# The end of a two-layer network on one core: last contexts kept in SBUF, the choice in two passes, eight groups of expert weights ahead, answers and tokens moved as groups end

## The chip, the cores and the metric

The kernel runs on one core of one Trainium2 chip. Its time is device time in microseconds (us) of one launch; "faster" and "slower" compare medians of such runs.

## What is computed

The input is four images of 64 x 64 positions with 128 channels, 4096 tokens an image. Two layers follow each other; the second has two parts, and the change lies at the end of the second part:

```python
x = x + L0(_gn(x))              # three selective scans (forward, backward, sliced)
t = _to_tokens(x)
t = t + L1_attn(_ln_t(t))       # attention, 16 heads of 8
t = t + L1_ffn(_ln_t(t))        # experts choose tokens
```

```python
# L1_attn, after q was made
scores = einsum('bhsd,bhtd->bhst', q, q) / sqrt(8); attn = softmax(scores)
attn_out = einsum('bhst,bhtd->bhsd', attn, q) @ w_comb.T + b_comb
x1 = _ln(x + attn_out, g1, beta1)
h = relu((cos(x1[..., :8]) * cos(ry_theta)) @ w1.T + b1)
return _ln(x1 + h @ w2.T + b2, g2, beta2)
# L1_ffn: 64 experts, each takes its 8 best tokens of an image
probs = softmax(x @ gate_w.T + gate_b, axis=1)      # over the tokens
vals, idx = top_k(probs, 8)
pooled = sum of the 8 tokens, weighted by vals
h = gelu([pooled, 1] @ weight1[e]); out = [h, 1] @ weight2[e]
outputs[idx] += out * vals
```

The expert weights are 64 x (128 x 512 + 512 x 128) numbers in float32, and each is used once.

## The kernel before, in words

The scans come first; their steps then run beside the attention of the image before. An image's attention is `Attention.loop`: a turn is a set j of four heads and a block qb of 512 queries, and in a turn 32 rounds go over 128 keys each. A round makes scores (L1013), takes their exponential on ACT (L1018), and adds the weighted values and the sum of the weights into `acc` (L1027). At the end of a turn `sums` copies `acc` to the tile `av` (L1036; two buffers), and three rounds later POOL's queue stores contexts (L1042) and denominators (L1045) to DRAM. Other work is put between the rounds by hand, through generators that yield where they may be interrupted. For the last image (index 3) the turns go block by block, and between the rounds stand, in this order: what follows image 2's attention, the expert biases, then for the pair of images 0 and 1 and for image 2 the experts' search, choice and gather, then the blocks 0 to 6 of image 3 (`after`), and a search over their logits. Only block 7 of image 3 remains when the loop ends.

`after` for a block: `shares` loads the denominators, inverts them (L1105) and stores them as shares (L1106). `first` loads the block's normed tokens (L1113), the contexts (L1115) and the shares spread over eight rows a head (L1117), multiplies (L1122), applies `w_comb` (L1130), norms (L893 to L899, with two small operations on POOL, L50 and L51), and stores x1. Then a sine (L1241), and `second`: x1 and t back from DRAM (L1146, L1148), transposes (L1153), h (L1171), fo (L1184), two norms, stores of t2 and xn (L1196, L1200), transposes (L1208), logits (L1222), which for this last block go straight into the tiles `prob` and `best` (L1226).

`choice` finds the eight best (L1321), takes the exponential of `prob` in place in four cuts with sums (L1331), replaces the eight best by -1 in a copy called `chosen` (L1335), and multiplies marks by exponentials (L1345): `chosen` then holds the weight where an expert chose a token and zero elsewhere. `gather` (`pool`) goes over blocks of 512 tokens, two at a time: load xn (L1352, SyncE's queue, four buffers), turn the weights by a matmul with a diagonal of the inverse sums (L1357), copy (L1363), pool (L1368), and add to `pooled` (L1374).

`answers`: groups of four experts, 16 groups of 2.1 MB of weights (L1385, L1388). A group is h (L1399), a copy on ACT (L1404), transposes (L1409), bias (L1412) and Gelu (L1417), o (L1422), and a copy into `o_all` (L1426). Two groups run side by side. Five groups are loaded ahead: one from POOL's queue before the last loop, three from ACT's queue as the loop ends, and one more from ACT's queue after block 7. A group that ends starts the load of the group five later from SyncE's queue. Twelve token tiles t (`DEEP`) are loaded from POOL's queue (L1455). After the last group the answers go to DRAM by image (L1473) and come back by expert (L1477), get bias and share, and `scatter` multiplies them with `chosen` for each block (L1491), adds t (L1498), and SyncE's queue writes the output (L1500); the next t load follows.

Of the kernel before, what the change touches and what calls it, by code (L numbers as in the profile page):

```python
# [34 lines left out]
QB = 512  # L35
F32R = mybir.dt.float32r


# [690 lines left out]
class Attention:  # L729
# [3 lines left out]
    def __init__(self, tc, ctx, w, gate, cols, ident, bank, dram, t1, w_out, scans, sz, x):  # L733
# [53 lines left out]
        self.u, self.q, self.v, self.context, self.total, self.t2 = {}, {}, {}, {}, {}, {}  # L787
        self.xn, self.logits, self.angled, self.whole, self.closed = {}, {}, {}, {}, {}
        self.lag, self.cut = 0, False
        self.round = column(nc, const, ROUND, "round"), column(nc, const, -ROUND, "minus_round")  # L790
# [172 lines left out]
    def loop(self, b, beside, by_block=False):  # L963
# [69 lines left out]
        def sums(j, qb, i):  # L1033

            av = self.mid.tile([P, QB], F32, tag="av", name=f"av_{b}_{j}_{qb}")
            (nc.vector.tensor_copy if by_block else nc.scalar.copy)(av, accs.pop((j, qb)))  # L1036
            cut = slice(qb * QB, (qb + 1) * QB)

            def store():
                for k in range(4):  # L1040
                    h = 4 * k + j
                    nc.gpsimd.dma_start(  # L1042
                        out=self.context[b][h * D : h * D + D, cut], in_=av[32 * k : 32 * k + D, :]
                    )
                nc.gpsimd.dma_start(  # L1045
                    out=self.total[b][qb].rearrange("(k j) t -> j k t", j=4)[j], in_=av[D::32, :]
                )
                if by_block and j == 3:
                    self.whole[b] = qb + 1

            later[i + 3] = store
# [22 lines left out]
    def after(self, b, gs=range(L // QB), to=None):  # L1074
# [173 lines left out]
        yield from flow((second(g) for g in gs), self.n, 32 // self.n)  # L1248


DEEP = 12


class Experts:
# [4 lines left out]
    def __init__(self, tc, ctx, ident, weight1, weight2, block, nb):  # L1259
# [14 lines left out]
        self.diagonal = const.tile([P, nb // 2, E], F32, name="diagonal")  # L1274
        self.found, self.ahead, self.rooms = {}, [], 0

# [17 lines left out]
    def search(self, images, blocks):  # L1294

        nc = self.nc
        rows = slice(images[0] % 2 * E, images[-1] % 2 * E + E)
        prob = self.const.tile([P, L], F32, tag="prob", name=f"prob_{images[0]}")
        best = self.some.tile([P, TOP + QB], F32, tag="best", bufs=1, name=f"best_{images[0]}")
        self.found[images] = rows, prob, best  # L1300
        while self.block.closed[images[-1]] < blocks:
            yield WAIT
        for b in images:
            own = slice(b % 2 * E, b % 2 * E + E)
            nc.sync.dma_start(out=prob[own, : blocks * QB], in_=self.block.logits[b][:, : blocks * QB])
        yield
        nc.vector.max(out=best[rows, :TOP], in_=prob[rows, : blocks * QB])
        yield
# [6 lines left out]
    def choice(self, images, blocks):  # L1315
# [10 lines left out]
        yield  # L1326
        nc.scalar.activation(top, top, AF.Exp, bias=low)
        total = some.tile([P, NC], F32, tag="total", name=f"total_{key}")[rows]
        for g in range(NC):
            cut = prob[rows, g * T : (g + 1) * T]  # L1330
            nc.scalar.activation(cut, cut, AF.Exp, bias=low, accum_out=total[:, g : g + 1])  # L1331
            yield

        w = self.chosen[key // 2][rows]
        nc.vector.match_replace(out=w, in_to_replace=top, in_values=prob[rows], imm_value=-1.0)  # L1335
        yield
# [3 lines left out]
        for b in images:  # L1340
# [3 lines left out]
            )  # L1344
        nc.vector.scalar_tensor_tensor(w, w, 0.0, prob[rows], ALU.is_lt, ALU.mult)  # L1345
        yield

    def pool(self, b, g):

        nc, bank, rows = self.nc, self.block.bank, slice(b % 2 * E, b % 2 * E + E)  # L1350
        x = self.some.tile([P, 4, C], F32, tag="x", bufs=4, name=f"x_{b}_{g}")
        nc.sync.dma_start(out=x, in_=self.block.xn[b][:, g * 4 : g * 4 + 4, :])  # L1352
        yield
# [11 lines left out]
        yield  # L1365
        ps = yield from bank.take(f"pool_{b}_{g}")
        for i in range(4):
            nc.tensor.matmul(ps[:, :E], x[:, i, :], wT[:, i, :], start=(i == 0), stop=(i == 3))  # L1368
# [9 lines left out]
    def gather(self, images):  # L1378
        yield from flow((self.pool(b, g) for b in images for g in range(NT // 4)), 2, 3)

# [11 lines left out]

    def answer(self, g, w, o_all, pool):

# [7 lines left out]
        yield  # L1402
        raw = pool.tile([P, 4, P], F32, tag="raw", name=f"hr_{g}")
        nc.scalar.copy(raw, ps.rearrange("r (p k) -> r k p", k=4))  # L1404
# [20 lines left out]
        yield  # L1425
        nc.vector.tensor_copy(o_all[:, g, :], ps[:, :C])  # L1426
        bank.leave()
# [7 lines left out]
    def prefetch(self, room, by):  # L1435

        pool, n = room
        for _ in range(n):
            self.ahead.append((self.weights(pool, len(self.ahead), by), pool))

    def answers(self, ctx, out):
        nc, tc, bank, nb = self.nc, self.tc, self.block.bank, self.nb
        once = ctx.enter_context(tc.tile_pool(name="e_once", bufs=1))
        pool = ctx.enter_context(tc.tile_pool(name="e_pool", bufs=2))
        deep = ctx.enter_context(tc.tile_pool(name="e_deep", bufs=DEEP))
        ng = E // GE
# [4 lines left out]

        def bring(i):
            b, g = tokens[i]
            t = deep.tile([P, 4, C], F32, tag="t", name=f"t_{b}_{g}")
            nc.gpsimd.dma_start(out=t, in_=self.block.t2[b][:, g * 4 : g * 4 + 4, :])  # L1455
            ts[b, g] = t

        o_all = once.tile([P, ng, C], F32, name="o_all")

        def group(g):  # L1460
            yield from self.answer(g, loaded.pop(g), o_all, pool)
            if g + n < ng:
                loaded[g + n] = self.weights(self.ahead[g % n][1], g + n, nc.sync)
            elif len(ts) < DEEP:
                bring(len(ts))

        yield from flow((group(g) for g in range(ng)), 2, 4)
        for i in range(len(ts), DEEP):
            bring(i)
        answers = [once.tile([P, C], F32, name=f"answer_{j}") for j in range(nb // 2)]  # L1470
        by_image = self.block.dram.tile([nb, E, C], F32, name="d_answers")
        for c in range(GE):
            (nc.sync, nc.scalar)[c % 2].dma_start(  # L1473
                out=by_image.rearrange("b (g c) o -> c b g o", c=GE)[c], in_=o_all[32 * c : 32 * c + nb]
            )
        for j in range(nb // 2):
            nc.sync.dma_start(out=answers[j], in_=by_image[2 * j : 2 * j + 2].rearrange("k e o -> (k e) o"))  # L1477
            nc.vector.tensor_add(answers[j], answers[j], self.bias_2)
            nc.vector.tensor_scalar_mul(answers[j], answers[j], self.share[:, j : j + 1])
        yield  # L1480

        def scatter(i):
# [13 lines left out]
            for (b, g), ps in zip(pair, banks):  # L1496
                t = ts.pop((b, g))
                nc.vector.tensor_add(t.rearrange("p t c -> p (t c)"), t.rearrange("p t c -> p (t c)"), ps)  # L1498
                bank.leave()
                nc.sync.dma_start(out=out[b].rearrange("(t p) c -> p t c", p=P)[:, g * 4 : g * 4 + 4, :], in_=t)  # L1500
                if i + DEEP < len(tokens):
                    bring(i + DEEP)
                i += 1
            yield
# [32 lines left out]
def tile_kernel(tc, ctx, x, in_proj_w, dirs, out_proj_w, attn, gate, weight1, weight2, out):  # L1537
# [82 lines left out]
    experts = Experts(tc, ctx, ident, weight1, weight2, block, nb)  # L1620
    experts.prefetch(experts.room(ctx, 1, "right"), nc.gpsimd)
    blocks = L // QB
    pairs = [(b, b + 1) for b in range(0, nb - 2, 2)] + [(nb - 2,), (nb - 1,)]
    with tc.manual_schedule():
# [6 lines left out]
            block.after(nb - 1, range(0, 4)), block.after(nb - 1, range(4, 6)), block.after(nb - 1, range(6, blocks - 1)),  # L1631
            experts.search(pairs[-1], blocks - 1),
        )
        block.loop(nb - 1, lambda i: last.turn(1.5, i % 3 > 0 or i > 830), True)
        last.rest()
        block.cut = False
    loop.close()
    with ExitStack() as end:
        block.bank = Bank(end.enter_context(tc.tile_pool(name="end_ps", bufs=7, space=PSUM)), 7)
        with tc.manual_schedule():  # L1640
            room = experts.room(end, 3)
            with ExitStack() as pieces:
                block.pieces_of(pieces, 1, opening=False)
                closing = block.after(nb - 1, range(blocks - 1, blocks), experts.rest(pairs[-1], blocks - 1))
                for i, _ in enumerate(closing):
                    if i == 2:
                        experts.prefetch(room, nc.scalar)
            experts.prefetch(experts.room(end, 1), nc.scalar)
            for _ in experts.choice(pairs[-1], blocks - 1):
                pass  # L1650
            for _ in experts.gather(pairs[-1]):
                pass
            for _ in experts.answers(end, out):
                pass
# [32 lines left out]
```

## Time and profile before

| | us |
|---|---|
| median of 3 runs | 11369.05 (11349.99 to 11371.47) |
| the profiled execution, its own time | 11359.39 |
| span of its trace | 11357.7 |
| busy: ACT, PE, DVE, POOL | 9991.9, 9864.2, 8267.2, 3757.7 |
| ACT's exponentials of the attention (L1018) | 7777.9 |
| last matmul of the attention ends | 11109.2 |
| first h of the answers starts (L1399) | 11229.2 |
| last addition of the output ends (L1498) | 11351.1 |
| moved from 11100 on | 53.04 MB |
| mean granted TensorE clock | 0.943 of full |

A row of a group of instructions gives the line, engine, operation, tiles out and in, shapes and count; then busy time and the mean of one in ns; then the engine's idle time just before them and what ended it. PE is TensorE's matmuls, PEld its weight loads; a float32 matmul is counted as two instructions. DVE is VectorE, ACT ScalarE, POOL GpSimd, and SPq, ACTq and POOLq are their queues of transfers. The granted clock is 1.00 at full speed. The time of the page is from the start of the span.

### The profile page before, as it was taken

To read this page: it belongs to the slowest core of one execution; us is meant where nothing else is said; L and a number is where in the kernel's file an instruction comes from. 1 tells how busy PE (TensorE), PEld (TensorE's weight loads), DVE (VectorE), ACT (ScalarE), POOL (GpSimd) and SP (SyncE) were. 2 spreads that over 40 slices of the span, in tenths; PEclk is the share of its full clock that TensorE was granted. 3 is DMA by queue.
4 is the path that set the end of the run, shared out by engine and by line. 5 is a ranking of instruction groups with operands and counts; after the bars stand their busy time and mean duration, and the time that the engine had idled before them with its cause. 6 is when DMAs were issued, how large, how long until landed. Compare 5 with 4: busy or idle time off the path is not lost.

```text
span 11357.7 us, 182956 instructions
## 1 busy us (share of the span) xinstructions
PE 9864.2 (87%) x68358; PEld 3270.5 (29%) x68358; DVE 8267.2 (73%) x8405; ACT 9991.9 (88%) x10828; POOL 3757.7 (33%) x3891
## 2 busy tenths in 40 slices
PE   6697782888999889999998898999998999999995
PEld 2233331222222222222222222222222223333323
DVE  7999987888888987999998979988999221111212
ACT  4576672999999999999999999999999999989992
POOL 5887773323323223334233124243331110000000
PEclk8898895999999999999999999999999999999997
DMA  7888887556566665665656655656555332222225
GB/s 200 235 253 228 231 239 206 147 144 156 140 155 164 178 171 140 158 164 136 156 140 172 185 158 153 156 140 153 148 146 156 119 99 71 76 71 83 76 64 187
DMA packets 900978, 1747.50 MB, mean 154 GB/s; under 512 B 203150, under 2 KB 443846, under 8 KB 899830
## 3 DMA queue, kind: packets, MB, share of 16 engines
q1 hardware_dynamic: 764414, 1468.11, 48.4%
q0 software_dynamic: 93856, 156.41, 4.8%
q10 hardware_dynamic: 41816, 111.28, 3.4%
q8 instruction: 537, 8.80, 0.3%
q14 instruction: 355, 2.91, 0.1%
HBM read 1379.76 MB, written 355.47 MB: 153 GB/s over the span
## 4 chain that ended last, share of the span: by engine, by line
PE 37%; ACT 25%; issue 14%; DVE 12%; DMA 10%; POOL 1%; SPq 1%; ACTq 0%; DVEq 0%; POOLq 0%
PE acc L1027 21%; ACT e L1018 20%; PE s L1013 10%; DVE h L576 5%; DMA delta<-d_delta 4%; DMA du<-d_du 2%; PE cv L415 2%; DVE dB L566 1%; ACT dA L557 1%; ACT delta L557 1%; PE y L614 1%; PE fo L1184 1%; PE h L1171 1%; PE xd L431 1%; DMA B<-d_bc 0%
## 5 line engine op out<-in xcount | busy, mean ns | idle before, releaser
L1018 ACT ACTIVATE e<-s 128x1024 f32<-128x1024 f32 x8192 | 7777.9, 1105 | 233.1 <-PE s L1013 221.3
L1027 PE MATMUL acc<-e,val 128*32 128x512 f32 x32768 | 5255.2, 616 | 106.7 <-ACT av L1036 94.0
L1013 PE MATMUL s<-qm,key 32*128 32x512 f32 x16384 | 2648.4, 500 | 588.5 <-ACT e L1018 558.4
L1013 PEld LDWEIGHTS s<-qm,key 32*128 32x128 f32 x16384 | 1013.8, 184 | 4448.8 <-issue 2490.0
L578 POOL COPY ends<-h 128x1 f32<-128x1 f32 x1152 | 1292.6, 1123 | 2332.1 <-DVE h L576 2318.1
L566 DVE TENSOR_TENSOR dB<-du,B 128x1024 f32<-128x1024 f32 x960 | 1216.0, 1267 | 450.8 <-PE y L614 224.7
L1027 PEld LDWEIGHTS acc<-e,val 128*32 128x32 f32 x32768 | 972.6, 109 | 1608.4 <-issue 787.9
L576 DVE TENSOR_TENSOR_SCAN h<-dA,ends,dB 128x1024 f32<-128x1024 f32 x576 | 1350.4, 2344 | 110.9 <-ACT dA L557 70.7
L557 ACT ACTIVATE dA<-delta,A 128x1024 f32<-128x1024 f32 x768 | 935.6, 1218 | 421.4 <-DMA delta<-d_delta 373.7
L576 DVE TENSOR_TENSOR_SCAN h<-delta,ends,du 128x1024 f32<-128x1024 f32 x432 | 1012.3, 2343 | 127.4 <-ACT delta L557 64.8
L583 POOL TENSOR_TENSOR hC<-h,C 128x1024 f32<-128x1024 f32 x384 | 1001.1, 2608 | 160.2 <-PE y L614 85.1
L557 ACT ACTIVATE delta<-delta,A 128x1024 f32<-128x1024 f32 x768 | 937.4, 1221 | 21.6 <-DMA d_du<-u 7.1
L587 DVE TENSOR_TENSOR du<-h,C 128x1024 f32<-128x1024 f32 x576 | 701.1, 1217 | 0.1
L587 DVE TENSOR_TENSOR dB<-h,C 128x1024 f32<-128x1024 f32 x576 | 701.0, 1217 | 0.0
L566 DVE TENSOR_TENSOR du<-du,B 128x1024 f32<-128x1024 f32 x576 | 690.6, 1199 | 6.0 <-DMA B<-d_bc 5.9
L1042 POOL DMA_DIRECT2D d_ctx<-av x512 | 260.2, 518 | 1020.8 <-DVE av L1036 647.0
L415 PE MATMUL cv<-xn,conv 128*128 128x512 f32 x1024 | 472.6, 615 | 41.8 <-DVE xn L346 31.7
L608 POOL DMA_DIRECT2D d_du<-x_delta x272 | 157.2, 578 | 1012.9 <-DVE x_delta L607 951.8
L576 DVE TENSOR_TENSOR_SCAN h<-dA,dB 128x1024 f32<-128x1024 f32 x192 | 438.7, 2285 | 40.7 <-ACT dA L557 30.4
L614 PE MATMUL y<-dB,sel 128*32 128x256 f32 x4608 | 378.5, 401 | 9.5 <-DVE xT L1211 5.1
L576 DVE TENSOR_TENSOR_SCAN h<-delta,du 128x1024 f32<-128x1024 f32 x144 | 328.8, 2283 | 67.4 <-issue 34.5
L614 PE MATMUL y<-hC,sel 128*32 128x256 f32 x3072 | 239.8, 443 | 147.9 <-DVE o L630 144.6
(246 smaller groups left out, 7198.1 us busy)
## 6 DMA issues: line engine op xcount, KB each, us to landing
delta<-d_delta SPq DMA_DIRECT2D x768, 512.0 KB
du<-d_du SPq DMA_DIRECT2D x632, 512.0 KB
key<-d_q SPq DMA_DIRECT2D x352, 256.0 KB
du<-d_du ACTq DMA_DIRECT2D x136, 512.0 KB
B<-d_bc SPq DMA_DIRECT2D x96, 512.0 KB
C<-d_bc SPq DMA_DIRECT2D x96, 512.0 KB
us<-d_u SPq DMA_DIRECT2D x384, 128.0 KB
y<-d_y SPq DMA_DIRECT2D x192, 256.0 KB
```

The lines of the kernel that those rows point to most:

```text
L415: nc.tensor.matmul(banks[2 * m + g], w["conv"][:, k, m * P : (m + 1) * P], reads(k, g), start=(k == 0), stop=(k == 3))
L557: nc.scalar.activation(tiles["delta", s], t, AF.Exp, scale=A)
L566: nc.vector.tensor_mul(tiles["du", s], du, spread[order, c, "B", j % 2])
L576: nc.vector.tensor_tensor_scan(h, dA, dB, first, ALU.mult, ALU.add)
L578: nc.gpsimd.tensor_copy(ends[order, c][:, at : at + 1], h[:, T - 1 :])
L583: nc.gpsimd.tensor_mul(tiles["du", s], h, spread[order, c, "C", j % 2])
L587: nc.vector.tensor_mul(dB, h, spread[order, c, "C", j % 2])
L614: nc.tensor.matmul(y[32 * g : 32 * g + 32, : T // 4], self.sel[:, j // 2, :], hC[:, 256 * g : 256 * g + 256], start=(j == 0), stop=(j == 3),)
L1013: nc.tensor.matmul(s_ps[:, k, :], keys[f"{i // 4}"][rows, cut].bitcast(F32R), queries[j, qb][rows, :].bitcast(F32R), start=True, stop=True,)
L1018: nc.scalar.activation(e, s_ps, AF.Exp, scale=1.0 / math.sqrt(D))
L1027: nc.tensor.matmul(accs[j, qb][32 * k : 32 * k + 32, :], v[:, k * VW : k * VW + 32], es[i][k // 2][:, k % 2, :], start=(kc == 0), stop=(kc ...
L1042: nc.gpsimd.dma_start(out=self.context[b][h * D : h * D + D, cut], in_=av[32 * k : 32 * k + D, :])
```

## The change

All of it concerns the last image's end, except that the choice for the other images changes its steps too.

- The contexts of image 3's block 7 are no longer stored: `sums` keeps the four `av` tiles (now four buffers). `combs` makes four copies of `w_comb` whose rows stand as the heads stand in `av`; `divide(j)` sums and spreads a tile's denominators by matmuls, inverts and multiplies in place. `combs` and `divide(0..2)` run between the rounds of the loop.
- `ending` replaces `after` for block 7: one pass without DRAM in between, activation tables loaded early, and 31 matmuls (`warm`) into a spare bank that nothing reads.
- `choice` writes exponentials to `chosen` and marks `prob`, and the marks are applied block by block as `pool` begins. `final`, for image 3, does the replacement beside a first set of exponentials that only give sums (into PSUM), and a second set in place; it turns weights one block ahead and sums all blocks in one bank.
- Weight groups 1 to 3 are loaded from SyncE's queue after the last division, 4 to 6 after `ending`, 7 after `final`. `prob` and `best` have a pool of their own that is given up for group 7.
- In `answers` three groups run side by side. As a group ends, four transfers from POOL's queue move its rows to their place in `answers` (for the last group two of them from ACT's). From group 8 on the room of a group's weights takes eight token tiles, from SyncE's queue; all 32 are loaded this way. The output leaves from SyncE's and ACT's queues in turn.

```diff
 def sums(j, qb, i):
+    if by_block and qb == L // QB - 1:
+        self.kept[j] = av
+        return
...
+def divide(self, j):
+    for i, cut in enumerate(halves):
+        for k in range(4):
+            one = self.ident[:, 32 * k + D : 32 * k + D + 1].to_broadcast([P, 32])
+            nc.tensor.matmul(ps[rows, cut], one, av[:, cut], start=True, stop=True)
+    for cut in halves:
+        nc.vector.reciprocal(r[:, cut], ps[:, cut])
+        nc.vector.tensor_mul(av[:, cut], av[:, cut], r[:, cut])
...
+def warm(self, n, by):
+    for i in range(n):
+        self.nc.tensor.matmul(self.spare, self.ident, by, start=True, stop=True)
...
+def ending(self, b, to, by, prefetch):
+    yield from self.divide(3)
+    prefetch()
+    nc.vector.tensor_add(u, u, spread("b_comb"))
+    for k in range(4):
+        for j in range(4):
+            nc.tensor.matmul(ps[:, at], self.kept[j][:, at], self.comb[:, j, :], start=(j == 0), stop=(j == 3))
+    self.warm(8, by)
...
+    self.warm(9, by)
+    yield from self.norm(u, u, f"x2{b}_{g}")
...
+    nc.tensor.matmul(ps[rows], self.gate, xT, start=True, stop=True)
+    self.warm(14, by)
...
+def final(self, images, blocks, by):
+    nc.vector.match_replace(out=w, in_to_replace=top, in_values=prob[rows], imm_value=GONE)
+    for g in range(n):
+        ps = yield from bank.take(f"exp_{g}")
+        nc.scalar.activation(ps[rows], prob[rows, cuts[g]], AF.Exp, bias=low, accum_out=total[:, g : g + 1])
+    for g in range(n):
+        nc.scalar.activation(prob[rows, cuts[g]], prob[rows, cuts[g]], AF.Exp, bias=low)
...
+    yield from turn(0)
+    for g in range(n):
+        if g + 1 < n:
+            yield from turn(g + 1)
+        x = self.xs.pop((b, g))
+        for i in range(4):
+            nc.tensor.matmul(sums[:, :E], x[:, i, :], wTs[g][:, i, :], ...)
+        if g + 4 < n:
+            self.tokens(b, g + 4)
...
 def group(g):
-    yield from self.answer(g, loaded.pop(g), o_all, pool)
+    o = pool.tile([P, C], F32, tag="o", name=f"os_{g}")
+    yield from self.answer(g, loaded.pop(g), o, pool)
+    for b in range(nb):
+        at = b % 2 * E + g * GE
+        by = (nc.gpsimd, nc.scalar)[b % 2] if g == ng - 1 else nc.gpsimd
+        by.dma_start(out=answers[b // 2][at : at + GE, :], in_=o[b::32, :])
     if g + n < ng:
         loaded[g + n] = self.weights(self.ahead[g % n][1], g + n, nc.sync)
-    elif len(ts) < DEEP:
-        bring(len(ts))
+    else:
+        bring(self.ahead[g % n][1], g)
...
-yield from flow((group(g) for g in range(ng)), 2, 4)
+yield from flow((group(g) for g in range(ng)), 3, 2)
```

## The prediction

> **What bounds the kernel now.** I read the page's rows by slices first, then the end of the run in stretches of 10 us, then the chain of waits in that stretch, then the groups by line. The page's slices (284 us each):
>
> ```profile
> PE   6697782888999889999998898999998999999995
> ACT  4576672999999999999999999999999999989992
> PEclk8898895999999999999999999999999999999997
> GB/s 200 235 253 228 231 239 206 147 144 156 140 155 164 178 171 140 158 164 136 156 140 172 185 158 153 156 140 153 148 146 156 119 99 71 76 71 83 76 64 187
> ```
>
> Up to the last slice ACT is full: the attention's exponentials (L1018, 7777.9 us) pace the run, and the change leaves nearly all of that alone. In the last slice ACT falls to 2 tenths and PE to 5. The change lives there: from the last matmul of the attention, at 11109.2, to the end of the span at 11357.7 are 248.5 us. Stretches of it (columns: length, busy time and instructions of PE, weight loads, DVE, ACT, POOL; granted clock; DMA share; GB/s):
>
> ```profile
> 11110.00:11120.00 10.00, 0.00 (x0) 0.00 (x0) 0.00 (x0) 0.00 (x0) 2.60 (x5) 0.72 1.00 349
> ...
> 11180.00:11190.00 10.00, 0.00 (x0) 0.00 (x0) 5.75 (x6) 4.15 (x8) 0.00 (x0) 0.50 0.99 362
> ...
> 11220.00:11230.00 10.00, 8.56 (x37) 7.31 (x40) 1.66 (x5) 0.00 (x0) 0.00 (x0) 0.50 0.00 0
> ...
> 11250.00:11260.00 10.00, 6.68 (x103) 3.18 (x105) 2.66 (x5) 3.12 (x6) 0.00 (x0) 1.00 1.05 387
> ...
> 11300.00:11310.00 10.00, 1.08 (x32) 0.81 (x32) 0.29 (x1) 0.63 (x1) 0.00 (x0) 0.77 0.10 13
> ```
>
> No one limit holds. Until 11230 it is a chain of latencies with the clock at half; in the experts' answers the transfers are full (387 GB/s); around 11305 nothing runs. The chain of waits (start, us, what):
>
> ```profile
> 11112.19 5.45 DMA d_sum<-av
> 11118.20 4.93 DMA x<-d_un
> 11124.22 5.64 DMA d_share<-sum
> 11130.37 3.43 DMA part<-d_share
> ...
> 11265.50 9.02 DMA w<-in_L_ffn_weight_dram
> ```
>
> The first four are round trips through DRAM for one 512-token block; the last is the answers waiting for weights. And the gather's groups, from the groups by line of this stretch (busy, mean ns | idle before):
>
> ```profile
> L1368 PE MATMUL pool<-wT,x 128*128 128x64 f32 x64 | 15.7, 427 | 4.1 <-DVE wT L1363 4.1
> L1357 PE MATMUL wt<-diagonal,chosen 64*128 64x64 f32 x64 | 15.7, 424 | 18.3 <-DVE chosen L1345 18.3
> ```
>
> **Part one: from the last context to the last block's logits.** Before, from the copy of the last sums (L1036, 11109.23) to `low` (L1325, ending 11177.75) are 68.5 us. Removed are the stores, loads and shares between 11109.92 and 11133.99, 24.1 us. Added in their place: eight matmuls that sum and spread the denominators, four at a time side by side, half of them ahead of DVE (0.7 us, from the answers' h of the same packing, 0.9 to 1.0 us for twice the columns); two reciprocals of 128x256 (the same shape took 1.75 us in L1105) and two multiplications (0.42); b_comb added (0.69). The combination has 16 matmuls instead of 4: at the transposes' 0.66 us for four at full clock 2.6 us, at the old row's 2.05 us for four at half clock 8.2 us; half of them lie on the path, 1.3 to 4.1.
>
> Behind that the rows of before repeat: a norm is 1.75 (statistics) + 1.43 (POOL) + 1.12, spreads are 0.7 each, h was 7.19 us and fo 5.83 us mostly at half clock. L1137 and L1138 (1.4) move behind the sine. With a full clock (h 3.6, fo 2.6) I add up: first halves divided and combined by 11116.3, norm 11121.5, sine 11123.5, h 11128.9, fo 11132.4, two norms with their spreads 11143.7, logits 11147.6, `low` 11148.6. I put 3 us on this for a clock that sags between, so 11151.5: **26 us gained**. If it is half throughout, 9 us more of matmul time.
>
> The fillers (8, 9 and 14 matmuls of 128x512 on nothing) stand in PE's queue before needed work. At about 0.9 us each at full clock (the answers' h has the same columns) they last 7.2, 8.1 and 12.6 us. The first gap is 7.4 us, the second 10.4: covered. The third is not: from the logits DVE and ACT need about 9.5 us, so PE is late by 3. At half clock the fillers would take 14.4, 16.2 and 25.2, which is the second rival.
>
> Weights: groups of 2.1 MB (23.07 MB in eleven by the transfers' view). Groups 1 to 3 leave SyncE's queue instead of ACT's, behind two 256 KB loads of this block, near 11111 as before, and take 16.3 us at 387 GB/s; nobody waits on them. Groups 4 to 6 wait until the block's last store (2.4 us) frees its buffers, near 11149, done by 11167. Behind them in the same queue stand the gather's token loads 4 to 7, each also held by a pool step; the first is wanted near 11170. That is cover of 3 us, so I charge nothing, and 3 if it goes. Group 7 stands behind those. The Trainium skill ("DMA: Bandwidth & Descriptors", Issuing engines are not separate DMA queues) says that spreading over queues saves only issue time; the out transfers now leave from two queues. Rows of one queue already moved 359 to 370 GB/s there, so I take 0 by both.
>
> **Part two: choice and gather.** Before, `low` to the first h (11229.2) 51.4 us: a table load and exponentials 6.4, replacement 4.5, marking 4.4 after it, 16 blocks of PE work at 2.19 us with the waits between. After: replacement (4.5) runs beside the first exponentials (eight of 512, about 0.7 by L1331's 1.13 for 1024, so 5.6), the second eight (0.6 each) run ahead of DVE, marks come by 512 (0.6) under PE. So PE may start about 7 us behind `low`; the fillers end at 11161.6 in my sum. Sixteen blocks then run in a row: 1.97 us each by the row at clock 0.50, 0.97 if weight loads halve as those of hT did (0.42 against 0.72 for four).
>
> Which? The Trainium skill ("TensorE: Matmul & The Clock Gate", What's actually happening) says sustained busy work of about 3.4 us opens the clock and an idle window closes it. By that the gather after fillers runs at full: 15.5 us. But the row contradicts it: 36 us of these same blocks, PE busy 85%, never left 0.50, while fo opened it in 4.2 us; and at 11285 it closed when PE was busy 0.54 us in 2. Narrow matmuls seem not to count enough. I take 5 us at full (five blocks), then eleven at 1.97: 26.7 us, bounds 15.5 and 31.5. First h at 11188: **15 us gained**.
>
> **Part three: answers, moves, output.** Before: 128.5 us, which is eleven groups at 385 GB/s (59.9) begun late, 21 us from 11297 to 11318 almost without transfers (answers out and back through DRAM, 8.8 us at L1478), then 13.6 MB at 365 GB/s (37). After: eight groups are ahead, 16.8 MB of weights remain, 43.5 us; 8.4 MB of tokens and 8.4 MB of output, 45.4 us at 370. Before only 20 tokens loads were left here, now all 32: that is in the sum. The first w2 load waits for the first o, 7 us in, with 1 MB (2.7) ahead of it; the tail after the last transfer is about 1. So 88.9 + 4.3 + 1 = **94 us, 34 gained**.
>
> What lies beside: three groups side by side take about 8.2 us by rows (h 0.95, copy 0.59, hT 0.66, add 0.69, Gelu 0.63, o 1.08), 2.7 a group against 4.0 before, faster than weights come (5.4): PE is not the bound. The last answer leaves about 6 us behind the last weights, its rows land perhaps 5 later, scatter starts near 60 us; DVE needs 32 x 0.7 = 22. Tokens keep the transfers full until 70, so 10 us of slip are hidden. Four row moves a group go to POOL (0.5 each, 2 us a group), replacing its token loads. New wait: the copy of an answer waits until the rows of the group three back have landed; behind it on DVE stands the next bias add, and Gelu and o wait for that.
>
> **In the loop.** Comb transposes 0.7, three divisions with 0.9 of PE each: 3.5 us on a PE that is 10.00 of 10 busy there. Rounds with such extras near 10940 took 2.07 against 1.83, so it can cost all; bounds 0 and 4, I take 3. DVE's reciprocals, marks in eight parts (0.5 more per pair) and the 15 stores gone have free engines (DVE 2 tenths); if that cover were gone, 15 us.
>
> **Sum.** 26 + 15 + 34 - 3 = 72 to 73. Span 11357.7 gives 11285; the profiled execution's own 11359.4 gives 11287; the median 11369.05, 9.7 us above it, gives **11296**.
>
> **Rivals.** (a) The clock stays full through the gather: first h at 11175, 11278 at the median. For it: fillers; against: the gather's row. (b) The clock is half in part one: fillers overrun by 7, 6 and 16 us, matmuls cost 9 more, the gather 5, less the 3 and 3 counted: 37 us back, 11333. Against: a filler run is itself dense enough to open it in 4 us. (c) Slower: the row moves. An answer copy is free while landing takes under 13 us (three groups are 16.3 us, less issue). Beyond, each of five turns adds the excess: at 28 us the gain is gone, at 32 it is 0.2% slower; at 34 it would be 11400. The trace's POOL transfers landed in 5.4 us (16 KB) beside flowing weights and 7.1 at worst (256 KB). (d) It doesn't do what it says: group 4 on is held by buffers or the queue, so answers starve as now. Parts two and three then yield 20 instead of 49: 11325.
>
> **How the numbers follow.** Forecast 0.52, (a) 0.20, (b) 0.10, (d) 0.08, (c) 0.06, and 0.04 for a wait I don't see that eats the gain. Faster and slower are counted beyond 0.2%, about what can be told from no change: faster 0.90, same 0.04, slower 0.06. The range reaches to (a) with good transfers, 11272, and to near (b), 11328.
>
> **What would show it.** Right: no DRAM leg between the last copy and the combination; `low` near 11150; first h near 11188 with the clock falling inside the gather; no group but the last ones waiting for weights; transfers without a hole between weights, tokens and output. Wrong: the attention's loop ending later by more than 5 us, clock 0.5 under the fillers, POOL's row moves over 13 us, a hole ahead of the output.

## The result, and the profile after

| | before | after |
|---|---|---|
| median on one chip, us | 11366.49 (4 runs, 11349.99 to 11371.47) | 11303.59 (4 runs, 11288.04 to 11304.78) |
| ratio, 95% interval | | 0.9945 (0.9931 to 0.9959) |
| profiled execution, its own time; span | 11359.39; 11357.7 | 11302.84; 11301.0 |
| last attention matmul ends (T below) | 11109.17 | 11107.57 |
| `low` done, after T | 68.6 | 42.9 |
| first turned weights of the gather start, after T | 84.5 | 54.1 |
| first h of the answers, after T | 120.0 | 84.6 |
| first scatter matmul, after the first h | 82.5 | 63.5 |
| last addition, after the first h | 121.9 | 89.7 |
| end of the span, after the first h | 128.5 | 108.8 |
| from T to the end | 248.5 | 193.4 |

The kernel became 63 us faster (47 to 78 by the interval of the ratio); 11296 was forecast, 11303.6 came. On two more chips the ratio was 0.9944 (0.993 to 0.9958) and 0.9946 (0.9934 to 0.9959), and in two more traces of the changed kernel T to the end was 193.4 and 193.2. So the tail, the time from T to the end, can be read to about 1 us, while T itself moved between 11091 and 11120 from one trace of any version to the next. I compare tails, and times only where medians stand on one chip.

The page's slices of the kernel after:

```profile
PE   6697782888989889999998898999998999999998
ACT  4576672999999999999999999999999999999994
PEclk8898895999999999999999999999999999999998
GB/s 200 237 252 226 229 240 204 148 149 155 142 154 156 179 171 147 159 157 144 151 147 159 195 156 155 158 142 148 147 143 173 129 93 71 69 85 81 71 73 187
```

The last digits changed: PE from 5 to 8, ACT from 2 to 4, the clock from 7 to 8. The rest is as before, to within a digit or a few GB/s. Stretches of the end (length; busy time and instructions of PE, weight loads, DVE, ACT, POOL; clock; DMA share; GB/s):

```profile
11110.00:11120.00 10.00, 8.39 (x41) 5.38 (x40) 7.46 (x18) 0.00 (x0) 1.23 (x2) 1.00 1.02 361
...
11130.00:11140.00 10.00, 10.00 (x38) 6.93 (x37) 4.15 (x16) 0.27 (x2) 1.21 (x2) 0.81 0.04 15
...
11170.00:11180.00 10.00, 10.00 (x44) 9.41 (x44) 2.65 (x5) 0.00 (x0) 0.00 (x0) 0.50 0.19 61
...
11210.00:11220.00 10.00, 8.62 (x147) 4.59 (x140) 3.15 (x7) 3.58 (x7) 7.69 (x14) 1.00 1.06 382
...
11250.00:11260.00 10.00, 6.23 (x71) 5.71 (x73) 3.26 (x8) 0.00 (x0) 1.89 (x4) 0.50 0.71 229
...
11290.00:11300.00 10.00, 0.00 (x0) 0.00 (x0) 0.00 (x0) 0.00 (x0) 0.00 (x0) 0.50 0.97 270
```

Right after T the engines now work beside the transfers, where before the transfers ran and PE and DVE stood idle. The gather (11170) is a PE that is full for all 10 us at half clock. Weights come at 382 GB/s. Then two things that the forecast did not have: a dip in the transfers near 11255, and a last stretch with nothing but output, at 270 GB/s with the DMA share still 0.97. The chain of waits (start, us, what):

```profile
11109.56 1.77 DVE part L1295
...
11113.96 1.40 PE co L1330 x10
...
11148.08 13.66 PE spare L1308 x28
11161.74 1.05 PE wt L1566 x8
...
11252.56 2.38 DMA answer<-os
11255.68 10.12 PE sc L1698 x136
...
11275.75 5.36 DMA t_w<-d_t
```

No round trip through DRAM is left before the combination. The third filler run stands on the chain, up to the first gather matmul, and at the end the chain waits for token loads. The groups of the end (busy, mean ns | idle before):

```profile
L1579 PE MATMUL pool<-wT,x 128*128 128x64 f32 x64 | 15.5, 427 | 0.0
L1566 PE MATMUL wt<-diagonal,chosen 64*128 64x64 f32 x64 | 14.3, 395 | 1.2 <-DVE chosen L1562 1.2
```

The idle time before the gather's matmuls went from 22.4 us to 1.2; their durations hardly changed, so the gather now is PE time at half clock. Last, SyncE's queue from 11185 on (us, times, longest):

```profile
...
SPq L1666 <- DMA out_dram<-t_w: 7.1, 3, 5.9
SPq L1591 <- DVE chosen L1562: 6.5, 1, 6.5
SPq L1591 <- PE h L1605: 6.0, 1, 6.0
...
SPq L1594 <- PE o L1628: 4.2, 1, 4.2
...
SPq L1666 <- DMA answer<-os: 2.8, 1, 2.8
```

L1666 loads tokens into rooms that no output or answer row uses, yet it stood 7.1 us for output transfers and 2.8 for the last rows, both issued by ScalarE. The operands in the trace show why. A transfer tells of its landing by a semaphore (a counter that others can wait for), and in this program those of SyncE and ScalarE take the same eight in turn (100 and 102 to 108), those of GpSimd eight others (111 to 118). Before a load leaves, SyncE waits for the semaphore that the load itself will use. So the load at 11254.32 waited 2.77 us for semaphore 107, in use by an answer row that ScalarE had issued at 11252.30, and the load at 11264.36 waited 5.87 us for 100, in use by an output of 11259.07. L1594 loads the second weight of a group and stood 4.2 us for the first o, with the next group's first weight behind it.

### The profile page after: what moved, and what is told of

It reads as the page before. It is cut to its first block, busy times and chain, and to the rows that moved or that the text cites. A ratio compares the mean times of both kernels' runs of the same rounds, so it can differ in the third digit from the quotient of the medians.

```text
span 11301.0 us, 183306 instructions
## 1 busy us (share of the span) xinstructions
PE 9870.8 (87%) x68502; PEld 3268.8 (29%) x68502; DVE 8278.3 (73%) x8437; ACT 9998.6 (88%) x10844; POOL 3797.9 (34%) x3900
## 4 chain that ended last, share of the span: by engine, by line
PE 37%; ACT 24%; issue 14%; DVE 12%; DMA 10%; POOL 1%; SPq 1%; ACTq 0%; DVEq 0%; POOLq 0%
PE acc L1029 21%; ACT e L1020 20%; PE s L1015 10%; DVE h L577 5%; DMA delta<-d_delta 4%; DMA du<-d_du 2%; PE cv L416 2%; DVE dB L567 1%; ACT dA L558 1%; ACT delta L558 1%; PE y L615 1%; PE fo L1189 1%; PE h L1176 1%; DMA d_y<-o 1%; PE xd L432 1%
## 5 line engine op out<-in xcount | busy, mean ns | idle before, releaser
L579 POOL COPY ends<-h 128x1 f32<-128x1 f32 x1152 | 1324.7, 1151 | 2303.8 <-DVE h L577 2288.9
L416 PE MATMUL cv<-xn,conv 128*128 128x512 f32 x1024 | 470.9, 613 | 42.9 <-DVE xn L347 31.8
L51 POOL TENSOR_TENSOR rs_x<-mv_x,eps 128x4 f32<-128x4 f32 x96 | 94.4, 983 | 911.1 <-DVE mv_x L896 911.0
## 6 DMA issues: line engine op xcount, KB each, us to landing
us<-d_u SPq DMA_DIRECT2D x384, 128.0 KB
```

Source lines behind the costliest of these rows:

```text
L416: nc.tensor.matmul(banks[2 * m + g], w["conv"][:, k, m * P : (m + 1) * P], reads(k, g), start=(k == 0), stop=(k == 3))
L579: nc.gpsimd.tensor_copy(ends[order, c][:, at : at + 1], h[:, T - 1 :])
```

## The experiments

The tails of all twelve, beside before and after (us; the last column is the median or, where one run is given, that run):

| | `low` after T | first h after T | end after first h | T to end | time |
|---|---|---|---|---|---|
| before | 68.6 | 120.0 | 128.5 | 248.5 | 11366.49, chip A |
| after | 42.9 | 84.6 | 108.8 | 193.4 | 11303.59, chip A |
| outs_other_queue | 42.0 | 83.9 | 105.5 | 189.4 | 11282.51, one run, chip B |
| gather_fill | 44.6 | 99.5 | 108.0 | 207.5 | 11310.81, one run, chip B |
| context_dram | 71.0 | 111.5 | 110.4 | 222.0 | 11312.03, chip B |
| five_ahead | 42.8 | 84.5 | 125.5 | 209.9 | 11305.03, chip B |
| after_again | 42.0 | 83.9 | 109.5 | 193.4 | 11291.79, chip C |
| warm_none | 47.1 | 86.3 | 108.3 | 194.6 | 11294.85, chip C |
| warm_ten | 43.0 | 81.3 | 109.3 | 190.6 | 11284.46, chip C |
| split_first | 42.8 | 84.5 | 104.3 | 188.8 | 11288.43, chip C |
| all_three | 42.0 | 78.4 | 100.8 | 179.2 | 11293.96, chip D |
| ten_split | 42.0 | 78.4 | 104.7 | 183.1 | 11298.67, chip D |
| after_third | 42.0 | 83.8 | 109.4 | 193.2 | 11303.70, chip D |
| before_again | 68.5 | 120.0 | 128.0 | 248.0 | 11346.47, one run |

The kernel before had a median of 11349.07 on chip B (8 runs), 11356.11 on C (9) and 11366.4 on D (9).

My theory after the first look: part one is as forecast; the gather is PE at half clock; the rest of the shortfall lies in the order of SyncE's queue, where loads and outputs stand behind waits that aren't theirs. The rival: the transfers themselves, or the answers' row moves, bound the end.

**context_dram.** The last contexts go through DRAM again, with the old step behind the loop; `combs` and `divide` are out of the loop, and with `ending` the fillers are gone too.

```diff
-if by_block and qb == L // QB - 1:
-    self.kept[j] = av
-    return
...
-experts.search(pairs[-1], blocks - 1), block.combs(...),
-*(block.divide(j) for j in range(3)),
+experts.search(pairs[-1], blocks - 1),
...
-closing = block.ending(nb - 1, experts.rest(...), ..., lambda: experts.prefetch(room, nc.sync))
+closing = block.after(nb - 1, range(blocks - 1, blocks), experts.rest(pairs[-1], blocks - 1))
+for i, _ in enumerate(closing):
+    if i == 2:
+        experts.prefetch(room, nc.sync)
```

> Part one alone is undone: the last block's contexts and denominators go through DRAM again and the old block code with its second DRAM round trip and without fillers follows; everything behind it is as changed. Theory (the parts add): from the last attention matmul to low 66 to 70 us instead of 42.9, the gather at half clock from its start (8 x 3.9 = 31.5 us), part three as changed at 105 to 110; the median 25 to 30 us above the changed kernel's, 11329 to 11334. Rival (transfers bound the end as a whole, so that what part one gains is given back later): the median within 10 us of the changed kernel's. The end of the attention loop, without the transposes and divisions between its rounds, tells what those cost: 0 to 3 us earlier.

Measured: `low` at T + 71.0, first h 26.9 us later than in the kernel after, and the end after the first h within 2 us. The time's ratio to before is 0.9966 (0.9952 to 0.998). The round trip is back in its chain:

```profile
11101.33 5.67 DMA w<-in_L_ffn_weight_dram
11107.02 7.51 DMA w<-in_L_ffn_weight_dram
11114.54 7.90 DMA part<-d_share
...
11123.40 2.06 PE co L1132 x8
```

Here the block's own small loads also stand behind three groups of weights that SyncE's queue now carries. What part one gives arrives at the end in full: nothing later swallows it.

**five_ahead.** Three of the eight groups are not loaded ahead.

```diff
-experts.prefetch(experts.room(end, 3), nc.sync)
```

> Groups 4 to 6 are no longer loaded ahead: five groups instead of eight, as before the change; token loads then take the rooms of groups 11 to 14. Theory (weights are the answers' bound): 6.3 MB more follow the first h, 16 us at 385 GB/s; first h to end 122 to 127 us instead of 108.8, first h itself unchanged, median 11318 to 11322. Rival (the side-by-side groups or the moved rows are the gain, not the loads ahead): first h to end within 4 us of 108.8.

Measured: the same first h, but the end 125.5 us after it instead of 108.8. PE's waits in the answers rose from 6.4 us in 2 to 19.1 in 6:

```profile
PE h L1605 <- DMA w<-in_L_ffn_weight_dram: 19.1, 6, 5.1
```

The three groups are 6.3 MB, 16.5 us at 380 GB/s; the end came 16.6 later. The time's ratio to before is 0.9961 (0.9946 to 0.9975). So eight groups do stand there in time, and in the answers each group not loaded ahead costs its transfer. That excludes the rival that later groups are held and the answers starve.

**gather_fill.** A matmul of 128x256 on nothing (it computes nothing that is used) behind each turn and each pooling step, so that PE has no gap and more columns.

```diff
+nc.tensor.matmul(self.block.spare[:, :256], self.ident, by[:, :256], start=True, stop=True)
```

> In the last image's gather one filler matmul of 128x256 on nothing follows each turn of weights and each pooling step (16 in all). Theory (narrow matmuls do not keep the clock open): the clock stays at 1.00 through the gather, a block step costs 0.97 plus 0.43 instead of 1.97, and from the first turn to the first h it is about 23 us instead of 30.5. Rival (the clock falls whatever is added, or the steps are not paced by the clock): the clock reads 0.50 from about 4 us on and the fillers add 0.9 each, 38 to 45 us.

Measured: from the first turned weights to the last pooled product 42.8 us instead of 30.2, the clock at half from 2.9 us on until the answers' h:

```profile
11170.00:11180.00 10.00, 10.00 (x38) 8.28 (x36) 2.23 (x4) 0.00 (x0) 0.00 (x0) 0.50 0.16 52
11180.00:11190.00 10.00, 10.00 (x36) 8.19 (x36) 1.79 (x4) 0.00 (x0) 0.00 (x0) 0.50 0.08 26
```

PE is busy 10.00 of 10 us for four such stretches, at 0.52 of the clock in the first and at half in the other three. The extra matmuls made the gather 12.6 us longer and opened nothing.

**warm_none.** The three `warm` lines are taken out; they compute nothing that is used.

```diff
-self.warm(8, by)
...
-self.warm(9, by)
...
-self.warm(14, by)
```

> All three filler runs are left out (they compute nothing that is used). Theory A, the fillers only keep the clock up while they run and cost 4 to 5 us where the third one outlasts its gap: the last block's projections run at half clock (low some 3 to 6 us later than T+42.9), the gather starts 4 us sooner after that, all its 16 blocks take 1.97 us (about 31 us), first h at T+82 to T+87, the time within 3 us of the changed kernel. Theory B, full clock is an allowance that the fillers use up before the gather: the gather keeps full clock for five blocks or more as in the kernel before (27 us or less), first h at T+70 to T+78, the time 7 to 14 us lower. Theory C, the fillers are worth what they are put there for: low 8 us or more later, the time 5 us or more higher.

Measured: `low` 4.2 to 5.1 us later than in the three traces of the kernel after, the gather's start at the same place (T + 54.4 against 53.9 to 54.1), the tail 1.2 to 1.4 longer, the time the same within its spread (11294.85 against 11291.79).

```profile
11126.99:11136.99 10.00, 0.42 (x4) 0.23 (x3) 6.63 (x24) 0.00 (x0) 2.76 (x5) 0.66 0.07 27
...
11166.99:11176.99 10.00, 10.00 (x45) 9.41 (x44) 3.34 (x6) 0.00 (x0) 0.00 (x0) 0.50 0.15 52
```

Theory A is what came: the fillers speed up part one by some 5 us and give back 4 where the third run outlasts its gap. In part one it is h above all that they speed up (3.7 to 4.1 us instead of 7.2); fo took 6.7 us without them and 5.4 to 6.6 in the three traces with them. The gather takes 31.5 us at half clock without them, and with them the clock is full for its first 2.9 to 3.7 us only, so they use up no allowance.

**warm_ten.** The third filler run is cut to the gap.

```diff
-self.warm(14, by)
+self.warm(10, by)
```

> The third filler run is cut from 14 to 10 groups of two (20 matmuls where 28 stood), so that it ends about when the chosen weights are there; it computes nothing that is used. Theory A (the overhang is 4 to 5 us on the path): the first gather transpose starts 3 to 5 us sooner against the low context, first h at T+80 to T+82, the time 3 to 5 us lower. Rival (the shorter run lets the clock fall before the gather): the gather's blocks all take 1.97 us instead of the first few at full clock, pool ends no sooner, the time unchanged within 2 us.

Measured: first h at T + 81.3 instead of 83.8 to 84.6; the tail 190.6, 2.6 to 2.8 shorter. The gather still took 30.3 us. The medians differ by 7.3 us, which their spread (5 runs each; the means differ by 2.1 us, with a 95% interval of about 11 us to either side) can't confirm; the traces show where the tail is shorter.

**split_first.** A group's first weight is loaded as soon as its buffer's matmuls are issued, and the second after the whole answer; the load of eight groups later is cut in two for that. In `answer`, `first()` stands behind the matmuls of h.

```diff
+def first():
+    if g + n < ng:
+        w1s.append(self.weights_1(self.ahead[g % n][1], g + n, nc.sync))
-yield from self.answer(g, loaded.pop(g), o, pool)
+yield from self.answer(g, loaded.pop(g), o, pool, first)
...
+first()
...
-loaded[g + n] = self.weights(self.ahead[g % n][1], g + n, nc.sync)
+loaded[g + n] = w1s[0], self.weights_2(self.ahead[g % n][1], g + n, nc.sync)
```

> The load of a group's first weight (w1 of the group eight later) is issued as soon as that buffer's matmuls are issued, ahead of the wait for the second weight's buffer; in the changed kernel w1 and w2 of a group are issued together after the whole answer, and SyncE holds the next w1 behind w2's wait. Theory (the answers are bound by weight transfers, which run at 90 to 290 GB/s in the first 16 us after the first h where 380 are possible): about 700 KB more move in that stretch, the end comes 2 to 6 us sooner after the first h than 108.8, transfers at 380 GB/s by 8 us after the first h. Rival (the loss is PE's: the first h matmuls and their half clock): no change within 1 us.

Stretches of 4 us from the first h, the kernel after ahead and this one behind it (clock, DMA share and GB/s stand last):

```profile
11196.20:11200.20 4.00, 4.00 (x81) 2.58 (x80) 2.37 (x4) 1.87 (x5) 0.45 (x1) 1.00 0.66 235
11200.20:11204.20 4.00, 3.57 (x65) 1.74 (x57) 0.58 (x2) 1.61 (x3) 4.00 (x8) 1.00 0.79 244
11204.20:11208.20 4.00, 4.00 (x81) 2.59 (x80) 2.35 (x4) 1.90 (x4) 2.33 (x6) 1.00 0.89 287
...
11252.20:11256.20 4.00, 0.52 (x3) 0.55 (x5) 1.21 (x5) 0.00 (x0) 1.10 (x2) 0.50 0.50 152
```

```profile
11186.43:11190.43 4.00, 4.00 (x78) 2.56 (x80) 2.32 (x4) 1.95 (x4) 0.34 (x1) 1.00 1.02 376
11190.43:11194.43 4.00, 3.57 (x65) 1.77 (x56) 0.63 (x3) 1.53 (x3) 4.00 (x8) 1.00 1.01 373
```

The transfers are full 4 us after the first h instead of 16, and the end comes 104.3 us after it instead of 108.8 to 109.5: 4.5 to 5.3 us, at the upper end of what was expected. The rival, PE's own start, is out. It speaks also against the answers' row moves as the bound: they are the same here.

**outs_other_queue.** ScalarE issues nothing any more: the last group's rows all leave from GpSimd, and the outputs from SyncE and GpSimd in turn.

```diff
-by = (nc.gpsimd, nc.scalar)[b % 2] if g == ng - 1 else nc.gpsimd
+by = nc.gpsimd
...
-by = (nc.sync, nc.scalar)[b % 2]
+by = (nc.sync, nc.gpsimd)[b % 2]
```

> Only the output transfers that left from ACT's queue, and the last group's two row moves there, leave from POOL's queue instead. Theory (shared completion counters): the token loads on SyncE's queue wait for counters that they share with ACT's transfers, and those wait for the answers' and the scatter's work; with POOL's transfers counted apart, the token loads run through without the holes at 11252-11256 and 11258-11264: all 32 issued within about 24 us of the first instead of 37, transfers near 380 GB/s between the last weights and the last token load, first h to end 100 us instead of 108.8. Rival (the room): the loads wait for the expert groups to give up their weights' room, or the transfers are full anyway; then the loads' issue still spreads over some 37 us and first h to end stays 107 to 110.

Measured: 105.5 us from the first h to the end, against 108.8 to 109.5. SyncE's waits from 11225 on:

```profile
SPq L1708 <- DVE t_w L1705: 13.6, 11, 3.4
SPq L1666 <- DMA t_w<-d_t: 7.8, 23, 0.7
SPq L1666 <- DMA w<-in_L_ffn_weight_dram: 3.9, 6, 2.3
```

No token load waits for an output or a row any more; SyncE is done with the loads early and waits for DVE's additions, as it should. No load of SyncE shares a semaphore with a transfer of ScalarE any more, since GpSimd's take 111 to 118. All 32 token loads left within 23.3 us, where they took 37 before, and the dip at the scatter's start is gone. But the last addition came no sooner (90.2 us after the first h): the scatter started 3 to 5 us later. The last o came 0.8 to 1.5 us later, and the last of the four row moves, which now leave one behind the other from one queue, 1.9 to 2.6. The gain is in the output behind it, 15.3 us instead of 19.1 (18.8 and 18.4 in the other two traces), and that runs at 263 to 290 GB/s. So the expected 100 us from the first h to the end did not come. The waits for ScalarE's transfers are worth 3 to 4 us; what lies above that is in good part the output's rate, and why output is slower than loads no run here shows.

**all_three, ten_split, after_third.** The last three edits together; the same without the outputs' edit; and the kernel after beside them.

> Three edits together: the third filler run cut to 20 matmuls (they compute nothing that is used), the first weights' loads issued ahead of the wait for the second weights' buffer, and the last group's rows and half of the outputs issued by GpSimd. If the three are different waits on one path they add: 2.8 + 5 + 3.5 = 11 us, tail from the last attention product to the end 182 us, first h at T+81, end 101 after it, the time 9 to 13 us below the changed kernel's on the same chip. Rival (the outputs' transfer at 270 to 340 GB/s bounds the end whatever comes before): first h and the last addition come sooner, the end by 5 us or less, tail 188.

> The same without the third edit (outputs and the last rows stay on SyncE's and ScalarE's queues). If they add: tail 185 to 186 us, end 104 after the first h, the time 7 to 8 us below the changed kernel's; the difference to the kernel with all three edits is then what the place of the outputs is worth, 3 to 4 us.

> The changed kernel as it is, on the same chip as the two others: tail 193.4 us, as in its two profiles so far; all theories.

Measured: tails 179.2, 183.1 and 193.2. The edits add, and 2 to 3 us more than expected came: the first h stood 5.4 us sooner than after_third's, where warm_ten alone had given 2.5 to 3.3. Against warm_ten the clock accounts for most of that: it was at half for 3.4 us of fo instead of 5.7 (`low` 1.0 us sooner) and at full for the first 5.2 us of the gather instead of 2.8 (28.7 us instead of 30.3). The outputs' place is worth 4.0 us. The times: all_three 11293.96 against 11303.70, mean difference 11.1 us with a 95% interval of about 2 to 20; its ratio to before is 0.9935 (0.9921 to 0.9948). ten_split is 5.0 below in the median, within the spread. all_three has the shortest tail and the lowest ratio of this study; what bounds it at the end is output alone (the engines' columns are empty):

```profile
11286.50:11290.50 4.00, 0.00 (x0) 0.00 (x0) 0.00 (x0) 0.00 (x0) 0.00 (x0) 0.50 0.97 277
```

**before_again.** The kernel before, for a second trace.

> The kernel before once more, for a second trace of it: its end and its last loop stand on one trace so far. If the prediction's base holds: 248 to 249 us from the last attention product to the end, and the loop of image 3 (first to last exponential) at 2034 us, against 2026 to 2036 in eleven traces with the combination's preparation between the rounds. Rival (the loop before is really some 8 us longer, as the medians less the tails suggest): about 2038 us or more, or an end of 241 us or less.

Measured: 248.0 from T to the end: the base of every difference here stands. The loop of image 3, from the first to the last of its 2048 exponentials, took 2031.2 us, in the first trace 2033.6, and 2029.6, 2029.5 and 2025.9 in the three traces of the kernel after. The rival's 2038 us did not come.

## Why the prediction was right, and where its steps were off

The direction and the range held; the time came 7.6 us above the forecast. That it came so near is partly luck: the tail fell 20 us short, and about 11 us of that were made up by the loop, which cost nothing visible where 3 us were charged, and by some 8 us that seem to have come ahead of T and that no term names. The base helped too: the median of before is 2.6 us lower with its fourth run. The forecast's steps beside the trace:

| step | forecast, us gained | measured in the trace |
|---|---|---|
| part one, T to `low` | 26 | 25.7 |
| part two, `low` to first h | 15 | 9.7 |
| part three, first h to end | 34 | 19.7 |
| sum of the tail | 75 | 55.1 |
| the loop | -3 | no cost seen; by medians about +8 |

**Part one** was right in sum: `low` at T + 42.9 where 42.3 was forecast, and context_dram shows that its 27 us are passed on to the end. Its terms were not all right, and fo was mis-sized twice. At full clock it was put at 2.6 us; the row of before, 5.83 us of which the first 4.2 ran at half clock, gives about 3.7 (4.2 / 2 + 1.6). And it didn't get the full clock. It took 6.6 us, nearly all of them in this stretch of the kernel after:

```profile
11127.10:11133.90 6.80, 6.80 (x30) 5.93 (x29) 0.42 (x1) 2.56 (x4) 0.00 (x0) 0.50 0.50 188
```

h took 4.1 us where 3.6 stood. The 3 us put on for a sagging clock and shorter norms covered all this. How long the half clock lasts there differs from trace to trace of the same code. In five traces it covered 3.4 us of fo, and `low` stands at T + 42.0; in four it covered 5.7 to 6.2, with `low` at 42.8 to 43.0; in gather_fill h fell into it too, and `low` came at 44.6. A difference of 1 us between two tails can be that alone.

The fillers took 7.0, 7.9 and 13.7 us, where 7.2, 8.1 and 12.6 stood, and "PE is late by 3" was right: warm_ten takes 2.6 to 2.8 off the tail. Rival (b), half clock in part one, came in part, for fo, and its 9 us were a fair size: in warm_none h and fo took 7.2 and 6.7 us, 7.7 more than the forecast's figures for full clock. The kernel after has some 4.5 of these itself, so that warm_none lost only 4 to 5 us up to `low` against it, and nothing behind `low`.

**Part two** failed in the step "I take 5 us at full (five blocks), then eleven at 1.97: 26.7". The clock was full for the first 2.9 us only: two blocks took 1.1 and 1.45 us and fourteen 1.97, and the gather 30.2 us. Beside that it began 11.2 us behind `low` and not 10.1. This was between the stated ends, near the slow one. The rule weighed there (the Trainium skill, "TensorE: Matmul & The Clock Gate", What's actually happening: some 3.4 us of sustained busy work opens the clock) is contradicted further by gather_fill: PE busy for 42.8 us, the last 39.9 of them at 0.50. "Narrow matmuls seem not to count enough" is neither shown nor excluded. For it: the gather's matmuls move 64 columns each (the rows of L1566 and L1579), while fo and the scatter, with 128 columns, and the answers' h, with 512, did open the clock; the scatter, with weight loads busy 4.00 of 4 us, came from 0.50 to 1.00 some 5 us after its start. Against it: the filled gather had 256-column matmuls in every block. What opens this clock stays open.

**Part three** failed in the sum "88.9 + 4.3 + 1 = 94". The bytes were right: 313 GB/s over 108.8 us is 34.1 MB, where 33.6 was counted. The rate was not held in three places, each set against the forecast's own rate:
- The first 16 us moved 3.4 MB, 8.9 us' worth at 385: 7.1 lost, 4.3 counted. The forecast saw that the first w2 waits for the first o, but charged it once; each w1 behind it in the queue waited too. split_first takes 4.5 to 5.3 off.
- From 11244 to 11276, at the step from weights to tokens, 9.5 MB took 32 us, 25.6 at 370: 6.4 lost, 0 counted. "Tokens keep the transfers full until 70, so 10 us of slip are hidden" was the wrong step: the token loads were held by the semaphores of ScalarE's transfers, and SyncE's outputs stood behind all 32 of them.
- From the last addition to the end 5.4 MB of output took 19.1 us, 14.5 at 370: 4.6 lost, 1 counted. The row of before that gave 365 GB/s mixed token loads with output; output alone runs at 345 falling to 270.

Beyond what was counted these are 2.8, 6.4 and 3.6 us, together 12.8 of the 14.8; the half MB moved beyond the count is 1.3 more. The outs on two queues were taken at 0, by the row and by the Trainium skill ("DMA: Bandwidth & Descriptors", Issuing engines are not separate DMA queues). For the rate that holds: moving them to GpSimd raised none. What neither told is that a queue's loads wait for another queue's transfers, 3 to 4 us. all_three gives a test of the sum: with both queue faults taken away the end came 100.8 us after the first h; the 6.8 us still above 94 are about the slow output, 18.4 us for 4.5 MB (12.1 at 370).

PE was indeed not the bound (6.4 us of waiting for weights, late), the eight groups were there (five_ahead), and row moves didn't hold the answers: a landing took 4.9 us in the median, the copies waited 15.9 us in 8 times, but the transfers were full at about 380 GB/s from 11208 to 11244 all the same. That leaves rival (c) without support. A trial with more answer buffers would have shown it directly and wasn't made. Nor was the two-pass choice, the third group side by side or the direct move of the rows taken back alone; what each of them gives is read from the traces, not shown by a run.

**The loop.** 3 us of cost were charged; image 3's loop took 2026 to 2030 us after and 2031 to 2034 before, so none is seen. More: on chips A, C and D the medians differ by 62.9, 64.3 and 62.7 us, some 8 more than the tails do, so about 8 us seem to have come ahead of T. Each of the three differences alone is uncertain by as much or more; that they agree speaks for it. The traces do not show them: T is 11109.2 and 11096.8 in the two of before, 11107.6, 11094.0 and 11108.7 in the three of after, and the profile of before was 7.1 us below its median. Where it lies I can't say. context_dram, with no preparation between the rounds, had the shortest loop of all, 2021.1 against 2025.9 to 2036.1 in eleven traces with it; if that holds, the preparation does cost some 8 us, and something else in the change, perhaps the choice or the missing stores, gives more than that back. It is one trace, so this stays open.

## What to carry to other kernels

Bytes divided by the best rate give a bound only if the queue that issues them never stands for another's sake: list, for each queue, which load stands behind which wait, and issue what is free ahead of what must wait. Look also at the semaphore that a load waits for before it leaves: transfers of another engine that take the same ones can hold it up without a common buffer. A stage that is moved off a round trip gives its whole length only if the next stage starts on it; here part one's 26 us passed through, while the gather's waits were replaced by PE's own time at half clock. Take the rate of a stream from a row that has only that stream in it: reads mixed with writes told nothing of writes alone.

## What the runs showed of the hardware that was not expected

- A PE busy for 10.00 of 10 us stayed at a granted clock of 0.50 for 39.9 us (gather_fill); in the changed kernels' gathers without fillers in between it was 23 to 32 us, whatever ran before (fillers, shorter fillers, none). The clock went to 1.00 some 3 to 5.5 us after the answers' h began, in every trace of a changed kernel.
- In all 14 traces the granted clock is either 0.50 or 1.00, and its changes lie whole multiples of 3.41 us apart (in the kernel after at 11127.07, 11133.90, 11147.55, 11150.96 and 11164.62). A mean between the two, as in a row of 10 us, is a mix.
- Output alone moved at 345 GB/s, falling to 270, with a DMA share of 1.15 to 0.97; issued by two other queues at 263 to 290 and a share of 1.0. Weights reached 380 at a share of 1.06. The DMA engines were busy and moved less.
- Token loads of SyncE's queue waited for output and row transfers of ScalarE's queue (7.1 and 2.8 us) though they share no buffer, because this program gives both queues the same eight semaphores; with nothing issued by ScalarE, these waits were gone.
